# A planned transformer block on one core: where the empty steps go, who adds one tile of exponentials, and where a square root stands

## The chip, the cores and the metric

The kernel runs on one core of one Trainium2 chip. The time is device microseconds (us) from launch to end, as the median of three runs. Engines are called PE (TensorE), ACT (ScalarE), DVE (VectorE), POOL (GpSimd) and SP (SyncE, which here only issues DMAs).

## What is computed

x has 4 sequences of 2,048 tokens of 512 numbers, all fp32. With xn = layernorm(x), the output is x + attention(xn) + ffn(xn):

```
qkv  = xn @ qkv_w.T + qkv_b            # 16 heads of 32
attn = softmax(q @ k.T * 32**-0.5)     # over 2,048 keys
att  = (attn @ v) @ proj_w.T + proj_b
idx  = top2(xn[:, 0, :] @ Wr + br)     # two experts of eight per sequence
ffn  = mean over the two experts of gelu(xn @ W1[e] + b1[e]) @ W2[e] + b2[e]
out  = x + att + ffn
```

## The kernel before, in words

**Units and chunks.** Attention is cut into 64 *chunks*: a sequence b (4), a group g of four heads (4) and 512 queries qc (4). A chunk has 16 *units*, kt = 0 to 15, one for each 128 keys; there are 1,024 units, numbered U (chunk U // 16). For the four heads of a unit, PE brings minus the row maximum into PSUM (`shift`, L773), adds the scores (`score`, L781), and ACT takes the exponential into a tile `pT[U]` of 128x2048 (L918). The maxima come from a first pass 22 units ahead (`score_max`, L763, reduced by DVE, L925). At every even unit `weigh` (L793) multiplies the two units before by v, and DVE adds the result to `sacc` (L802).

**The sum over keys.** The softmax denominator needs the sum of the 16 tiles `pT` of a chunk. `add_weights` has POOL add them into `psums` (L816 for the first two, L820 for the next thirteen), and the sixteenth by a DMA that adds, issued from POOL (L818). In the next chunk, at kt 4 or 5 (`plan.keys_at`), `add_keys` sums `psums` over partitions with four matmuls by a tile of ones (L826); ACT copies the result into `sums`, DVE inverts it in four parts, POOL multiplies (`divide`, L887). The tiles `pT` have four buffers: the exponential of unit U+4 needs the buffer of unit U. In the last chunk most tiles are summed by PE (`add_last`), a few by POOL (L809, L811).

**The layers in between.** Each odd unit has room for one step of the other work ("item"), 32 matmuls as a rule, 16 for the first two steps of a layer: q/k projections ("qk"), v, expert layers ("w1", "w2"), output projection ("proj"). "qk" and "w1" use seven products of half blocks in place of eight. These need sums of blocks of tokens ("tx") and of weights ("ws"), which POOL makes, four for each of 14 places, at the last unit of a chunk and the first two of the next. A finished half of an expert's hidden layer gets its gelu on ACT in the unit after the next item but one (`curves`, L922), with a table load before it and one back to exp after it. Rows of the first sequence get a bias from POOL (L953); for the others POOL issues DMAs that add it (L699).

**The planner.** `Plan` fixes the "qk" and "v" items (for each chunk group at written-out slots), then fills the other odd units from two queues with earliest times. There are more slots than items: what is spare is dealt out to slots with kt 5 ("rests"), as empty slots ("gaps"), except where a gelu is due. If the slot at kt 5 is empty, the keys of the chunk before are summed there, else at kt 4. "stats", "normal" and "turn" (layernorm and transposition of the next sequence) and "root" (its square root: ACT with two table loads, DVE reciprocal, two POOL operations, L452 to L455) have fixed units too. Root stands at unit 129, 385 and 641 for sequences 1, 2 and 3.

**The order on an engine** is the order of issue in the loop over U: shift and scores, exponentials, gelu, maxima, inversion, `add_weights`, `weigh`, `add_last`, `add_keys`, extra steps, item, stores, loads. PSUM is a ring of eight banks for all of it. In the last chunk `add_last` for an even unit comes two units later, or three if that slot is empty:

```
            late = u + 3 < plan.units and u + 3 not in plan.items
            if u % 2 == 0 and u >= plan.units - NT and late == (u == U - 3):
                add_last(u)
```

Of the kernel before, what the change touches and what calls it, by code (L numbers as in the profile page):

```python
# [37 lines left out]
class Plan:  # L38
# [3 lines left out]

    def __init__(self, B, DC, NCH, NT, TPC):
        self.per_group = NCH * NT
        self.per_seq = DC * self.per_group
        self.units = B * self.per_seq
# [10 lines left out]
        for G in range(1, B * DC):  # L59
            b, g = divmod(G, DC)  # L60
            first = (G - 1) * self.per_group
            for n, products in enumerate(GAPS):
                at = (11, 12, 13, 14, 15, 16, 17, 19) if g else (5, 6, 7, 8, 9, 11, 12, 13)
                fixed[first + 2 * at[n] + 1] = ("qk", b, g, products)
            if g == 0:
                at = [n for n in range(14, 32) if n % 8 != 2]
# [10 lines left out]
        for b in range(1, B):  # L77
            q1 = (b - 1) * self.per_seq + self.per_group
            q2 = q1 + self.per_group
            for k in range(TOP_K):  # L80
                at = q1 + ((NT - 1, q2 - q1 + 5 * NT - 1) if b > 1 else (-1, NT - 1))[k]
                for n in range(4):
                    self.extra.setdefault(at + COMBINED[n], []).append(("ws", b, (k, n)))
                for i in STEPS:
                    self.first_load["wt", ("w1", b, k, i)] = at + STORED + 1
            for n in range(NT):
                self.extra.setdefault(q1 + 2 * (16 + n) + 1, []).append(("stats", b, n))
                c, i = divmod(n, TPC)
                at = q2 + 2 * (1 + 18 * (c // 2) + 5 * (c % 2) + i) + 1
                self.extra.setdefault(at, []).append(("normal", b, n))  # L90
                self.extra.setdefault(at + 2, []).append(("turn", b, n))
            self.extra.setdefault(q2 + 1, []).append(("root", b, 0))
            for p in range(NCH // 2):
                at = q2 + 2 * NT * (p + 1) - 1
                for n in range(4):
                    self.extra.setdefault(at + COMBINED[n], []).append(("tx", b, (p, n)))
                for i in STEPS:
                    self.first_load["xt", (b, p, i)] = at + STORED + 1
                for c in (2 * p, 2 * p + 1):
                    self.first_load["xq", (b, c)] = at + STORED + 1  # L100
# [35 lines left out]
        todo = len(fixed) + sum(len(p) for _, p in ffn + proj)  # L136
        spare = len(slots) - todo - 4
        free = [s for s in slots if s > 0 and s not in fixed]
        rests = [s for s in free if s % NT == 5]
        share = spare / len(rests)  # L140
        current, before, owed = [], None, 0
        for s in slots:
            if s in fixed:
                self.items[s] = [fixed.pop(s)]
                before = None
                continue
            curve = before is not None and (
                before[0] == "w1" and before[4][-1] in ((3, 0), (3, 1), (2, 1))
                or before[0] == "w2" and before[3] % 2 == 1 and before[5] == 0
            )  # L150
            before = None
            if s in rests:
                owed += share
                if owed > 0 and not curve:
                    owed -= 1
                    continue
            if not current:
                for queue in (proj, ffn):
                    if queue and queue[0][0] <= s:
                        current = queue.pop(0)[1]  # L160
                        break
            if current:
                before = current.pop(0)
                self.items[s] = [before]
        self.keys_at = {}
        for s in range(NT, self.units, NT):
            ends = s + NT == self.units
            self.keys_at[s // NT - 1] = 5 if s + 5 not in self.items and not ends else 4
        assert not fixed and not proj and not ffn and not current, (proj, ffn, current)

        rows_at = {}
# [27 lines left out]
        for u in range(2, self.units + 1, 2):  # L199
            kt, G = (u - 2) % NT, (u - 2) // self.per_group  # L200
# [45 lines left out]
def block_kernel(  # L246
# [17 lines left out]
    B, N, D = x.shape  # L264
    E = Wr.shape[1]
    DC = D // P
    NT = N // P
    NCH = N // CH
    TPC = CH // P
    SCALE = float(HD) ** -0.5  # L270
    PSUM = bass.MemoryType.PSUM
    plan = Plan(B, DC, NCH, NT, TPC)
# [11 lines left out]
    def bank(name):  # L284
        return ps.tile([P, CH], F32, tag="bank", name=name)

    def rows_of(j):
        return slice(j * HD, (j + 1) * HD)
# [454 lines left out]
    def place(u):  # L743
        rest, kt = divmod(u, NT)
        rest, qc = divmod(rest, NCH)
        return (*divmod(rest, DC), qc, kt)

    mx, negm, sacc, psums, sums, pT = {}, {}, {}, {}, {}, {}
# [55 lines left out]
    def add_weights(u):  # L804
        b, g, qc, kt = place(u)
        if u >= plan.units - NT:
            if kt == 3:
                psums[b, g, qc] = pair.tile([P, GH, CH], F32, tag="psum", name="psum_last")
                nc.gpsimd.tensor_tensor(psums[b, g, qc], pT[u - 1], pT[u], ALU.add)  # L809
            elif kt in (5, 7, 9):  # L810
                nc.gpsimd.tensor_tensor(psums[b, g, qc], psums[b, g, qc], pT[u], ALU.add)  # L811
        elif kt == 0:
            return
        elif kt == 1:
            psums[b, g, qc] = pair.tile([P, GH, CH], F32, tag="psum", name=f"psum_{b}_{g}_{qc}")
            nc.gpsimd.tensor_tensor(psums[b, g, qc], pT[u - 1], pT[u], ALU.add)  # L816
        elif kt == NT - 1:
            nc.gpsimd.dma_start(psums[b, g, qc], pT[u], accum_op=ALU.add)  # L818
        else:
            nc.gpsimd.tensor_tensor(psums[b, g, qc], psums[b, g, qc], pT[u], ALU.add)  # L820

    def add_keys(where, ps, weights, again):

        for n, t in enumerate(weights):
            for j in range(GH):
                nc.tensor.matmul(  # L826
                    ps[rows_of(j), :], ones, t[:, j, :],
                    start=(n == 0), stop=(n == len(weights) - 1),
                )
        if again:  # L830
            nc.vector.tensor_tensor(sums[where], ps, sums[where], ALU.add)
        else:
            last = where == place(plan.units - 1)[:3]
            sums[where] = pair.tile(
                [P, CH], F32, tag="vrow" if last else "sums", bufs=2 if last else 1,
                name="sums_%d_%d_%d" % where,
            )
            nc.scalar.activation(sums[where], ps, AF.Identity)  # L838

    def add_last(u):  # L840
        where, kt = place(u)[:3], place(u)[3]
        if kt == 2:
            return
        weights = [pT[u]] if kt in (4, 6, 8) else [pT[u], pT[u + 1]]
        if kt == 12:
            weights.append(psums[where])
        add_keys(where, bank(f"keys_{u}"), weights, kt > 0)
# [50 lines left out]
    for U in range(-LEAD, plan.units):  # L898
        second = U >= 0
        first_pass = U + LEAD if U + LEAD < plan.units else None  # L900
        chunk, kt = divmod(U, NT)
        b, g, qc, _ = place(U) if second else (0, 0, 0, 0)
# [16 lines left out]
        curve = curves.pop(U, None)  # L919
# [14 lines left out]
        before = place(U - NT)[:3] if U >= NT else None  # L934
# [8 lines left out]
        two = any(it[0] in ("qk", "w1") and len(it[-1]) == 2 for it in plan.items.get(U, []))  # L943
# [6 lines left out]
        if second:  # L950
            add_weights(U)
# [7 lines left out]
        for u in (U - 2, U - 3):  # L959
            late = u + 3 < plan.units and u + 3 not in plan.items  # L960
            if u % 2 == 0 and u >= plan.units - NT and late == (u == U - 3):
                add_last(u)
        if before is not None and kt == keys:
            add_keys(before, bank("keys_%d_%d_%d" % before), [psums[before]], False)
        for step, sb, n in plan.extra.get(U, []):
            if step == "stats":
                if n == 0:
# [9 lines left out]
            else:  # L977
                c, i = divmod(n, TPC)
# [2 lines left out]
                if i == TPC - 1:  # L981
                    later(U + 1, lambda sb=sb, c=c, xs=xs: nc.sync.dma_start(xn_dram[sb, c], xs))
        for item in plan.items.get(U, []):
            dense(item, U, curve is not None, invert if two else lambda: None)


        for do in waiting.pop(U, []):
# [30 lines left out]
    U = plan.units  # L1018
# [78 lines left out]
```

## Time and profile before

| what | value |
|---|---|
| median of 3 runs | 4973.19 us (4972.93 to 4974.06) |
| profiled execution | 4967.9 us, of it 4966.1 us span and 1.8 us around it |
| granted PE clock | 0.999 |
| PE busy | 4913.9 us (99%) |
| POOL busy | 4403.5 us (89%) |
| DVE busy | 3714.2 us (75%) |
| ACT busy | 2491.9 us (50%) |
| POOL adds of pT, L820 | 819, 4547 ns each |
| DMAs that add pT, L818 | 63, 1,024 KB each, 8.6 us median from issue to landing |

Busy time and a wait must be told apart here: PE is booked busy nearly always, since its matmuls are pipelined, so a short wait shows better in the distance between units than in a busy share. The first matmuls of L773 in each unit mark its start; all 4,096 of them are in the trace.

### The profile page before, as it was taken

The numbers are of one execution on the slowest core, as the hardware profiler recorded it, in microseconds if no ns is written. First come the engines' busy times: TensorE is split into PE (matmuls) and PEld (weight loads), VectorE is DVE, ScalarE is ACT, GpSimd is POOL, SyncE is SP. The second block draws the span as 40 slices with busy tenths as digits, with TensorE's granted clock in tenths as the row PEclk, the third lists the DMA queues.
The fourth block names the chain that finished last, engine by engine and source line by source line (L and its number), as shares of the span: only waits on it lengthen the run. The fifth ranks groups of instructions, "written<-read, shape, count | busy, mean of one in ns | idle before, by whom it ended". The sixth has DMA issues, their size and how long they took to land.

```text
span 4966.1 us, 108027 instructions
## 1 busy us (share of the span) xinstructions
PE 4913.9 (99%) x44740; PEld 1712.0 (34%) x44740; DVE 3714.2 (75%) x5899; ACT 2491.9 (50%) x4570; POOL 4403.5 (89%) x1469
## 2 busy tenths in 40 slices
PE   8999999999999999999999999999999999999999
PEld 2333333333333333333333333333333333333332
DVE  5777787777777787777777778877777777777772
ACT  1445456464444545454455445555544445555553
POOL 2799999999898998999988998999988988989983
PEclk9999999999999999999999999999999999999999
DMA  6334337433333434634234244564423343323323
GB/s 225 113 106 120 112 99 196 150 121 110 82 107 104 131 109 139 187 122 137 88 94 132 73 128 128 171 167 131 145 70 98 106 129 107 95 81 112 87 81 101
DMA packets 327772, 594.93 MB, mean 120 GB/s; under 512 B 42220, under 2 KB 162540, under 8 KB 310384
## 3 DMA queue, kind: packets, MB, share of 16 engines
q1 hardware_dynamic: 311872, 509.37, 31.7%
q0 software_dynamic: 15408, 78.65, 8.2%
q8 instruction: 352, 5.77, 0.5%
q14 instruction: 140, 1.15, 0.1%
HBM read 380.81 MB, written 153.62 MB: 108 GB/s over the span
## 4 chain that ended last, share of the span: by engine, by line
PE 83%; ACT 6%; POOL 5%; issue 3%; DMA 2%; DVE 1%; SPq 0%; POOLq 0%; ACTq 0%
PE acc L793 17%; PE s L781 15%; PE m L763 15%; PE qkps L503 6%; PE ops L503 6%; PE hps L503 6%; PE s L773 6%; PE vps L503 5%; POOL psum L820 4%; PE prps L503 4%; ACT p L918 3%; DMA psum<-p 2%; PE keys L826 1%; ACT L692 1%; ACT h L922 1%
## 5 line engine op out<-in xcount | busy, mean ns | idle before, releaser
L820 POOL TENSOR_TENSOR psum<-psum,p 128x2048 f32<-128x2048 f32 x819 | 3724.0, 4547 | 158.3 <-ACT p L918 117.4
L918 ACT ACTIVATE p<-s 128x512 f32<-128x512 f32 x4096 | 2116.9, 602 | 2225.3 <-PE m L763 2062.8
L925 DVE TENSOR_REDUCE mx<-m 128x1 f32<-128x512 f32 x4096 | 2543.1, 683 | 569.2 <-PE m L763 567.4
L781 PE MATMUL s<-qT,kT 32*128 32x512 f32 x8192 | 1919.0, 588 | 0.0
L763 PE MATMUL m<-kT,qT 32*128 32x512 f32 x8192 | 1911.3, 590 | 3.9 <-DVE row L657 2.5
L763 PEld LDWEIGHTS m<-kT,qT 32*128 32x128 f32 x8192 | 921.8, 184 | 330.2 <-issue 240.5
L793 PE MATMUL acc<-p,v 128*32 128x512 f32 x8192 | 985.8, 599 | 9.6 <-ACT p L918 5.5
L781 PEld LDWEIGHTS s<-qT,kT 32*128 32x128 f32 x8192 | 768.1, 185 | 30.8 <-issue 9.2
L503 PE MATMUL ops<-wb_w,h 128*32 128x512 f32 x4096 | 466.0, 595 | 0.2 <-ACT p L918 0.2
L816 POOL TENSOR_TENSOR psum<-p,p 128x2048 f32<-128x2048 f32 x63 | 288.1, 4573 | 194.0 <-ACT p L918 194.0
L793 PEld LDWEIGHTS acc<-p,v 128*32 128x32 f32 x8192 | 214.0, 109 | 709.7 <-ACT p L918 392.8
L802 DVE TENSOR_TENSOR sacc<-acc,sacc 128x512 f32<-128x512 f32 x448 | 309.9, 692 | 139.9 <-PE acc L793 139.9
L773 PE MATMUL s<-negms,ones_b 32*128 32x512 bf16 x4096 | 406.2, 385 | 7.5 <-ACT p L918 7.0
L503 PE MATMUL hps<-xt,wt_w 128*32 128x512 f32 x3584 | 411.0, 596 | 1.1 <-ACT p L918 1.0
L773 PEld LDWEIGHTS <-ones_b 32*128 32x128 bf16 x4096 | 103.4, 91 | 858.0 <-issue 850.4
L503 PE MATMUL qkps<-xt,wt_qk 128*32 128x512 f32 x3360 | 386.7, 597 | 11.4 <-ACT p L918 11.4
L940 DVE RECIPROCAL sums<-sums 128x128 f32<-128x128 f32 x252 | 235.9, 936 | 0.7 <-ACT sums L838 0.7
L503 PEld LDWEIGHTS ops<-wb_w,h 128*32 128x32 f32 x4096 | 120.0, 109 | 314.7 <-issue 229.8
L657 DVE SCALAR_TENSOR_TENSOR row<-ops,row 128x512 f32<-128x512 f32 x128 | 88.5, 691 | 163.9 <-PE ops L503 153.6
L503 PE MATMUL prps<-wb_proj,xl_at 128*32 128x512 f32 x1792 | 203.9, 595 | 0.0
L503 PEld LDWEIGHTS hps<-xt,wt_w 128*32 128x32 f32 x3584 | 103.3, 109 | 276.2 <-issue 185.4
L503 PEld LDWEIGHTS qkps<-xt,wt_qk 128*32 128x32 f32 x3360 | 97.1, 110 | 283.6 <-issue 180.6
(127 smaller groups left out, 1975.6 us busy)
## 6 DMA issues: line engine op xcount, KB each, us to landing
xt<-t_dram SPq DMA_DIRECT2D x181, 512.0 KB
xt<-xn_dram SPq DMA_DIRECT2D x133, 512.0 KB
psum<-p POOLq DMA_DIRECT2D x63, 1024.0 KB, 8.6
part_dram<-row SPq DMA_DIRECT2D x128, 256.0 KB
v_dram<-v SPq DMA_DIRECT2D x64, 256.0 KB
wt_w<-ws_dram SPq DMA_DIRECT2D x128, 128.0 KB
v<-v_dram SPq DMA_DIRECT2D x64, 256.0 KB
row<-part_dram SPq DMA_DIRECT2D x64, 256.0 KB
```

Of the source, the lines that this page charges most:

```text
L503: nc.tensor.matmul(pp[rows_of(j), :], lhsT[:, rows_of(j)], rhs, start=(first and n == 0), stop=(last and n == len(terms) - 1),)
L657: nc.vector.scalar_tensor_tensor(row, pp, 0.5, row, ALU.mult, ALU.add)
L763: nc.tensor.matmul(t, qT[b, g, qc][r, ts(i, P)], kT[b, g, kc][r, :], start=True, stop=True)
L773: nc.tensor.matmul(tiles[j], ones_b[r, :], negm[b, g, qc][r, :], start=True, stop=False)
L781: nc.tensor.matmul(tiles[j], kT[b, g, kt // TPC][r, ts(kt % TPC, P)], qT[b, g, qc][r, :], start=False, stop=True,)
L793: nc.tensor.matmul(acc[r, :], held["v", (b, g, kt // TPC)][:, (kt + n) % TPC, r], pT[u + n][:, j, :], start=(n == 0), stop=(n == 1),)
L802: nc.vector.tensor_tensor(t, acc, t, ALU.add)
L816: nc.gpsimd.tensor_tensor(psums[b, g, qc], pT[u - 1], pT[u], ALU.add)
L820: nc.gpsimd.tensor_tensor(psums[b, g, qc], psums[b, g, qc], pT[u], ALU.add)
L918: nc.scalar.activation(pT[U][:, j, :], tiles[j], AF.Exp, scale=SCALE)
L925: nc.vector.tensor_reduce(dst, t, AX.X, ALU.max, negate=True)
L940: nc.vector.reciprocal(sums[before][:, q], sums[before][:, q])
```

## The change

1. **Gaps.** A chunk in whose first units POOL sums blocks ("ws" or "tx" that begin at the last unit of the chunk before) gets no gap at kt 5. There are twelve such chunks; the same number of gaps is dealt to the rest.
2. **One tile of chunk 62.** For unit 1007, the sixteenth of the last chunk but one, `add_weights` does nothing (no adding DMA). PE sums that tile over partitions by ones at unit 1008, ACT copies it into `sums`; at kt 4 or 5 the rest of the chunk is summed as ever and DVE adds it to `sums`.
3. **Roots.** If the planner finds a root in a slot that it marks as a gelu's, it plans once more with that sequence's root, normals and turns two units later. In a unit with a root the first evacuation of a "w1" layer, a copy, goes to DVE in place of ACT.

Worked through with this kernel's sizes, the slots change so (gaps at kt 5 by chunk, and the empty slots of the last chunk by unit):

| | before | after |
|---|---|---|
| chunks with a gap | 0 1 4 5 7 9 11 13 15 16 18 20 22 24 26 28 30 33 34 35 37 39 42 43 45 47 48 50 52 54 57 58 60 62 | 0 1 6 7 8 9 13 14 16 17 19 20 23 24 30 31 32 33 35 38 39 41 43 47 48 50 51 53 54 56 57 60 61 62 |
| chunks that sum blocks | 4 5 10 12 21 26 28 29 37 42 44 45 | the same |
| empty in the last chunk | 1011, 1021, 1023 | 1011, 1013, 1023 |
| root of sequences 1, 2, 3 | 129, 385, 641 | 129, 387, 641 |
| gelu units near the second root | 385, 387 | 385, 387 |

Most items stay or move one slot earlier (2 units); a few change places with others.

```diff
@@ Plan.__init__
-    def __init__(self, B, DC, NCH, NT, TPC):
+    def __init__(self, B, DC, NCH, NT, TPC, late=()):
...
-                at = q2 + 2 * (1 + 18 * (c // 2) + 5 * (c % 2) + i) + 1
+                at = q2 + 2 * (1 + (b in late) + 18 * (c // 2) + 5 * (c % 2) + i) + 1
...
-            self.extra.setdefault(q2 + 1, []).append(("root", b, 0))
+            self.extra.setdefault(q2 + 1 + 2 * (b in late), []).append(("root", b, 0))
...
-        rests = [s for s in free if s % NT == 5]
+        summed = {
+            (s + 1) // NT for s, steps in self.extra.items() for e in steps
+            if e[0] in ("ws", "tx") and s % NT == NT - 1
+        }
+        rests = [s for s in free if s % NT == 5 and s // NT not in summed]
         share = spare / len(rests)
-        current, before, owed = [], None, 0
+        current, before, owed, curved = [], None, 0, set()
...
+            if curve:
+                curved.add(s)
...
+        again = {
+            b for s, steps in self.extra.items() for kind, b, _ in steps
+            if kind == "root" and s in curved
+        }
+        if again and not late:
+            self.__init__(B, DC, NCH, NT, TPC, tuple(again))
+            return
@@ add_weights
+        elif u == plan.units - NT - 1:
+            return
         elif kt == NT - 1:
             nc.gpsimd.dma_start(psums[b, g, qc], pT[u], accum_op=ALU.add)
@@ the loop over U
+        ends_soon = U >= plan.units - NT
+        if ends_soon and kt == 0:
+            add_keys(before, bank("keys_%d_%d_%d" % place(U)[:3]), [pT[U - 1]], False)
         if before is not None and kt == keys:
-            add_keys(before, bank("keys_%d_%d_%d" % before), [psums[before]], False)
+            add_keys(before, bank("keys_%d_%d_%d" % before), [psums[before]], ends_soon)
...
-            dense(item, U, curve is not None, invert if two else lambda: None)
+            rooted = any(e[0] == "root" for e in plan.extra.get(U, []))
+            dense(item, U, curve is not None or rooted, invert if two else lambda: None)
```

## The prediction

> **What bounds the kernel now.** I read the page first (busy shares, chain), then ACT's waits, then the timeline around the longest of them, and last the distances between the first L773 matmuls of neighbouring units, all 1,024 of them.
>
> ```profile
> span 4966.1 us, 108027 instructions
> PE 4913.9 (99%) x44740; PEld 1712.0 (34%) x44740; DVE 3714.2 (75%) x5899; ACT 2491.9 (50%) x4570; POOL 4403.5 (89%) x1469
> ...
> L820 POOL TENSOR_TENSOR psum<-psum,p 128x2048 f32<-128x2048 f32 x819 | 3724.0, 4547 | 158.3 <-ACT p L918 117.4
> ...
> psum<-p POOLq DMA_DIRECT2D x63, 1024.0 KB, 8.6
> ```
>
> PE is the bound. The change removes no PE work, so it can only remove waits of PE. How much waiting is there? From the unit distances: an even unit takes 3.90 us when nothing disturbs it (478 of them), an odd one with a full item 5.61, with a half item (16 matmuls) or a gap 1.72 or 3.57 less, keys add 0.86. Against those numbers units 0 to 1022 lose some 80 us in all, of it 0.43 at each of the 33 gaps with keys at kt 5 (0.14 in the gap, 0.29 after it). The losses of half a us and more are few, and of three kinds.
>
> *Kind 1, the adding DMA.* The exponential at kt 3 needs the buffer of kt 15 of the chunk before, which the DMA reads:
>
> ```profile
> ACT p L918 <- DMA psum<-p: 33.9, 8, 8.4
> ```
>
> ACT's timeline at the last chunk, and then POOL's, show the worst case:
>
> ```profile
> 4870.41 2.06 ACT L918 ACTIVATE p<-s 128x512 f32<-128x512 f32 x4 [2.69 <-PE s L781]
> 4880.86 2.07 ACT L918 ACTIVATE p<-s 128x512 f32<-128x512 f32 x4 [8.39 <-DMA psum<-p]
> ```
>
> ```profile
> 4863.81 4.57 POOL L820 TENSOR_TENSOR psum<-psum,p 128x2048 f32<-128x2048 f32 x1
> 4868.67 0.87 POOL L818 DMA_DIRECT2D psum<-p  x1 [0.30 <-POOL psum L820]
> ```
>
> POOL issues the DMA 8.76 us after the exponential of unit 1007 ended (its *lag*), the chain of waits gives the DMA 12.09 us, and unit 1012 takes 12.20 us where 3.90 is its due: 8.30 lost. For the other chunks I set lag plus landing time beside the loss: 17.0 (chunk 60) loses nothing, 17.7 (37) 0.61, 17.9 (44) 0.78, 18.3 (57) 1.41, 18.8 (5) 1.70, 23.0 (28) 7.43. So **17.0 us is the allowance**; past it PE loses about the excess, a little more if it is large. Losses of this kind: 5: 1.70, 7: 3.70 (1.51 of it at unit 128, where POOL itself is late), 9: 1.11, 22: 1.17, 28: 7.43, 37: 0.61, 42: 0.81, 44: 0.78, 57: 1.41; sum 18.7, and 8.30 at the end.
>
> *Kind 2, root with gelu*, ACT at unit 385:
>
> ```profile
> 1951.28 1.28 ACT L922 ACT_TABLE_LOAD   x1
> 1952.58 1.06 ACT L922 ACTIVATE h<-h 128x1024 f32<-128x1024 f32 x1
> 1953.65 1.28 ACT L692 ACT_TABLE_LOAD   x1
> 1954.95 0.20 ACT L692 ACTIVATE unused<-ones 128x1 f32<-128x1 f32 x1
> 1955.17 1.28 ACT L452 ACT_TABLE_LOAD   x1
> 1956.46 0.31 ACT L452 ACTIVATE sd<-mv,eps 128x16 f32<-128x16 f32 x1
> 1956.79 1.28 ACT L692 ACT_TABLE_LOAD   x1
> 1958.08 0.20 ACT L692 ACTIVATE unused<-ones 128x1 f32<-128x1 f32 x1
> ```
>
> Seven us between two exponentials; unit 386 loses 3.31. Unit 388, after a gelu with a normal, loses 0.81.
>
> *Kind 3, DVE or ACT crowded*: units 102 (0.78), 106, 378 and 618 (1.25 each) after "w1" or "qk" steps with three DVE evacuations beside statistics or an inversion; 380, 620, 142, 434, 654 (0.77 to 0.87) around gelus.
>
> **The change, part by part.**
>
> *Chunk 62 by PE.* Taken away: DMA and POOL's issue. At unit 1008 four matmuls come (eight records): 0.86 us by the L826 rows of the same size. They wait for nothing new: `weigh` ahead of them in unit 1008 already reads tile 1007. The ACT copy (0.60 to 0.63 us, L838) queues ahead of exponential 1009, where ACT idles 0.97; if that cover were gone it would cost its length. The DVE add takes 0.69 (L831) in place of the copy at kt 4, ahead of the inversion at kt 5, with DVE mostly idle there. POOL's last add ends at 4868.37, so keys at kt 4 (4875) find it done. The wait of 8.30 goes; next late is exponential 1010's buffer, free 2.0 us before its need. So −8.30 + 0.86 = −7.4.
>
> *The gap at 1013 in place of 1021.* At 1021 two postponed tiles of `add_last` (1.72 us of PE) fill the gap; at 1013 the postponed call is the one for kt 2, which does nothing. PE then has only 1.19 us in that unit, while ACT needs 2.06 for each exponential: `weigh` at 1014 waits for exponential 1013. ACT starts 1.34 after a unit's start, so 1012 runs 1.34 to 3.41 and 1013 to 7.30; PE gets there at 3.90 + 1.19 + 1.19 = 6.27: 1.0 to 1.15 lost (between 0 if banks let PE run differently, and 2.1, one whole exponential). I take +1.1. **Tail: −6.3.**
>
> *Gaps moved.* A gap shortens a chunk by 3.57 − 0.43 = 3.1 us net (0.4 is spent again on the gap itself) and adds about that to POOL's lag if POOL is busy throughout. What the gaps themselves cost, and the total of gaps, is as before. By chunk, lag from a running sum (old lag + POOL's work − PE's time), landing as measured before in that chunk:
> - 28 (four half items, token blocks): before 2.1 + 77.6 − 66.9 = 12.8; after, 3.3 longer without its gap, 9.5; landing 10.2: excess 6.0 → 2.7; loss 7.4 → 3.4.
> - 5: no gap in 4 and 5, lag 10.7 → about 5: 1.70 → 0. 37: 9.0 → 6: 0.61 → 0. 42: 0.81 → 0.
> - 22 loses its gap without summing blocks: landing was 12.0, lag 4.3 → 2.5: 1.17 → 0.
> - 7: row biases on POOL, one or two 1.3 us adds fewer, as they move to 6; chunk 1.7 shorter by a half item. Lag 9.9 → 8.2 to 9: 3.7 → 0.7.
> - 9 keeps its gap, but 8 gets one: lag 7.5 → 8.5: 1.1 → 2.1.
> - 41 gets a gap and has the bias DMAs as 9 has: before 5.0 + 77.3 − 76.4 = 5.9; after 3.2 (chunk 40 has 1.8 more PE work) + 77.3 − 72.8 = 7.7; landing 10.6: 0 → 1.2. Bounds: 0, and 3.1 (its whole lost length).
> - 38 gets a gap, landing there was 13.2: 0 → 0.9. 44 and 57 stay: 0.8 and 1.4.
> New sum 10.5 against 18.7: **−8.2**. Landing times are the weak point: they ran from 6.9 to 13.2 us and depend on loads that move. Bounds −12 and −2.
>
> *Roots.* The plan moves root 2 from 385 to 387, but the gelu's second half stands at 387 in both plans: root again follows a gelu, the same 6.9 us, and the loss of 3.31 moves to unit 388. Gained is only that the normal leaves that unit: −0.8. [...] The row shows the load alone; gelu starts 0.02 us after it. [...] With root really apart it would be −3.3 by the row. The copy on DVE at 129 and 641 (about 0.7 us by L657, in place of 0.6 on ACT behind root's 3.1 us) lies under a half item of 1.86 us: 0, bounds ±0.7.
>
> *Items one slot earlier.* Units 102, 106 and 620 lose their crowding (−2.5); similar steps land beside inversions or gelus in chunks 5, 29 and 37 and at 431; nearest rows 0.26 to 0.87 each: +2.3. Six more xt or wt loads of the plan's 869 are on SP; xt loads issued two units before use occur in both plans (six before, two after), and no unit of before waits on one; two wt loads become that short: 0, bounds 0 and +3. **Together with roots −1.0**, bounds −4 and +4.
>
> **Sum.** −6.3 − 8.2 − 1.0 = −15.5. The profiled execution, 4967.9 (span 4966.1 + 1.8), would take 4952.4. The median runs 5.3 above the profiled one, so I predict 4957.7, rounded to **4958**.
>
> **The rivals.** About 0.2% (10 us) is what this kernel's measurement can tell from no change: faster means below 4963.2, slower above 4983.1.
> - A, as summed, 4953 to 4963: 0.52.
> - B, only the tail pays; new landings and crowding take back what the gaps give: 4973.2 − 6.3 = 4967: 0.18. For it: landing varies by 6 us from chunk to chunk. Against: the 28, 5 and 37 sums are large.
> - C, more: landings are shorter once POOL is on time, and crowding leaves without coming back: −6.3 − 12 − 4 gives 4951: 0.15.
> - D, the tail does not do what it says: the wait at 1012 is taken over by another buffer or bank. Then −8.2 − 1.0 + 2.0 gives 4966: 0.08. Against: the next buffer is free 2 us early.
> - E, slower: POOL's lag carries from gap to gap. After, 16 gap chunks directly follow another gap chunk, before 7 (1 and 62 aside). If POOL no longer caught up at each chunk's head, each could lose 1.6: 16 × 1.6 = 26, giving 4984. It decides once lag at a chunk's end exceeds some 9 us, for then POOL's idle time before the add at kt 1 (3 to 9 us now) is gone. Against: 34, 35 and 48 follow a gap chunk and lag 4.4, just like 18 and 30. 0.07.
>
> So faster 0.67, same 0.26, slower 0.07. Range 4950 to 4967: A, most of C, and B and D to their middle.
>
> **What would show it.** Unit 1012 at 3.9 us, no ACT wait of 8 us on psum<-p, 62 such DMAs; unit 1014 about 1 us long over its due. Unit 467 loses 2.7 to 4, 99 and 371 nothing, 675 about 1. Unit 388 loses 3.3: if it doesn't, my reading of the roots is wrong. I am wrong if L918's waits on psum<-p stay above 25 us in all, or if new units with 2 us and more appear in chunks 6 to 9, 31 to 33 or 38 to 41.

## The result, and the profile after

The changed kernel takes 4964.54 us (median of 16 runs, 4959.88 to 4967.52) against 4973.48 us before (16 runs, 4970.38 to 4978.18): ratio 0.998, interval 0.9974 to 0.9987. That is 8.9 us or 0.18% less, inside the range of the prediction and somewhat over half of the forecast 15.5. It is above the 4963.2 below which the prediction would have called the kernel faster: the case "same", to which it gave 0.26. The profiled execution took 4965.18 us, 4963.4 of it span.

First the page of the changed kernel. Its lines have moved: L933 is the exponential, L835 POOL's add, L833 the adding DMA, L806 `weigh`, L516 the items, L465 to L468 root, L937 the gelu.

```profile
span 4963.4 us, 108069 instructions
PE 4916.5 (99%) x44748; PEld 1713.5 (35%) x44748; DVE 3717.3 (75%) x5904; ACT 2489.0 (50%) x4566; POOL 4402.9 (89%) x1468
...
L835 POOL TENSOR_TENSOR psum<-psum,p 128x2048 f32<-128x2048 f32 x819 | 3724.4, 4547 | 155.7 <-ACT p L933 114.7
...
psum<-p POOLq DMA_DIRECT2D x62, 1024.0 KB, 8.5
```

One DMA and one POOL issue fewer, eight matmul records more, and otherwise the same shares: a page cannot tell such kernels apart. ACT's waits and its timeline at the tail can:

```profile
ACT p L933 <- DMA psum<-p: 20.4, 6, 5.9
```

```profile
4875.91 2.07 ACT L933 ACTIVATE p<-s 128x512 f32<-128x512 f32 x4 [2.69 <-PE s L794]
4878.94 2.06 ACT L933 ACTIVATE p<-s 128x512 f32<-128x512 f32 x4 [0.97 <-PE s L794]
```

These are the exponentials of units 1010 and 1011, whose starts stood 10.45 us apart before and stand 3.03 apart now. The stretch from unit 1008 to the end (the tail) went from 104.87 to 97.51 us. But the waits on the DMA fell by 13.5 us in all, more than the tail gave, and the longest left is 5.9. It is new, at unit 131, in the head of chunk 8; the prediction had named a new loss of 2 us or more in chunks 6 to 9 as a sign that it is wrong. The changed kernel's timeline there, POOL's issue, then ACT, then PE:

```profile
751.80 0.86 POOL L833 DMA_DIRECT2D psum<-p  x1 [0.30 <-POOL psum L835]
...
761.89 2.07 ACT L933 ACTIVATE p<-s 128x512 f32<-128x512 f32 x4 [5.92 <-DMA psum<-p]
762.54 5.34 PE L516 MATMUL hps<-xt,wt_w 128*32 128x512 f32 x32 [4.01 <-ACT p L933]
```

PE waits 4.0 us, and then its 32 matmuls take 5.34 in place of 3.64. The losses of units against their due, found as in the prediction, in two profiles of each kernel (the second ones come with the experiments):

| units | before | before, again | after | after, again |
|---|---|---|---|---|
| 88 and 600 | 0 | 0 | 3.75 | 3.75 |
| 99 | 1.70 | 1.85 | 0 | 0 |
| 102, 106, 620 | 2.80 | 2.81 | 1.13 | 1.12 |
| 128, 130, 131 | 3.78 | 3.88 | 6.92 | 8.01 |
| 371 | 1.17 | 1.20 | 1.65 | 1.34 |
| 386, 388 | 4.12 | 4.12 | 5.00 | 5.11 |
| 399, 400 | 1.10 | 1.56 | 2.71 | 2.79 |
| 467 | 7.43 | 8.93 | 4.26 | 1.00 |
| 642, 643 | 0.07 | 0.07 | 1.21 | 2.72 |
| all of units 1 to 1007 | 71.2 | 73.0 | 75.2 | 73.6 |
| unit 1008 to the end | 104.87 | 105.71 | 97.51 | 97.51 |

So in the profiles the tail gave what the change gave, and over the first 1,008 units gains and losses cancel.

### The profile page after: what moved, and what is told of

Same layout as the page of the kernel before. It is cut to its first block, busy times and chain, and to the rows that moved or that the text cites. A ratio compares the mean times of both kernels' runs of the same rounds, so it can differ in the third digit from the quotient of the medians.

```text
span 4963.4 us, 108069 instructions
## 1 busy us (share of the span) xinstructions
PE 4916.5 (99%) x44748; PEld 1713.5 (35%) x44748; DVE 3717.3 (75%) x5904; ACT 2489.0 (50%) x4566; POOL 4402.9 (89%) x1468
## 4 chain that ended last, share of the span: by engine, by line
PE 86%; ACT 6%; POOL 3%; DMA 2%; issue 1%; DVE 1%; SPq 0%; POOLq 0%; ACTq 0%
PE acc L806 18%; PE s L794 16%; PE m L776 15%; PE qkps L516 7%; PE hps L516 7%; PE ops L516 6%; PE s L786 6%; PE vps L516 5%; PE prps L516 4%; POOL psum L835 3%; ACT p L933 3%; PE keys L841 1%; DMA psum<-p 1%; ACT L705 1%; ACT h L937 1%
## 5 line engine op out<-in xcount | busy, mean ns | idle before, releaser
L835 POOL TENSOR_TENSOR psum<-psum,p 128x2048 f32<-128x2048 f32 x819 | 3724.4, 4547 | 155.7 <-ACT p L933 114.7
L933 ACT ACTIVATE p<-s 128x512 f32<-128x512 f32 x4096 | 2116.6, 602 | 2227.7 <-PE m L776 2076.3
L806 PE MATMUL acc<-p,v 128*32 128x512 f32 x8192 | 986.7, 599 | 11.2 <-ACT p L933 7.3
L516 PE MATMUL ops<-wb_w,h 128*32 128x512 f32 x4096 | 466.0, 595 | 0.5 <-ACT p L933 0.5
L806 PEld LDWEIGHTS acc<-p,v 128*32 128x32 f32 x8192 | 214.2, 109 | 710.8 <-ACT p L933 395.6
L516 PE MATMUL hps<-xt,wt_w 128*32 128x512 f32 x3584 | 412.7, 598 | 5.7 <-ACT p L933 5.7
L516 PE MATMUL qkps<-xt,wt_qk 128*32 128x512 f32 x3360 | 387.0, 598 | 5.2 <-ACT p L933 2.7
L516 PEld LDWEIGHTS ops<-wb_w,h 128*32 128x32 f32 x4096 | 120.0, 109 | 315.0 <-issue 229.9
L516 PE MATMUL prps<-wb_proj,xl_at 128*32 128x512 f32 x1792 | 203.9, 595 | 0.2 <-ACT p L933 0.2
L516 PEld LDWEIGHTS hps<-xt,wt_w 128*32 128x32 f32 x3584 | 103.7, 110 | 282.9 <-issue 186.5
L516 PEld LDWEIGHTS qkps<-xt,wt_qk 128*32 128x32 f32 x3360 | 97.5, 110 | 276.4 <-issue 180.3
```

Source lines behind the costliest of these rows:

```text
L516: nc.tensor.matmul(pp[rows_of(j), :], lhsT[:, rows_of(j)], rhs, start=(first and n == 0), stop=(last and n == len(terms) - 1),)
L806: nc.tensor.matmul(acc[r, :], held["v", (b, g, kt // TPC)][:, (kt + n) % TPC, r], pT[u + n][:, j, :], start=(n == 0), stop=(n == 1),)
L933: nc.scalar.activation(pT[U][:, j, :], tiles[j], AF.Exp, scale=SCALE)
```

## The experiments

Times are medians; ratios are to the kernel before on the same chip, with their interval. Some kernels share the same runs of before. Times of versions that did not run together compare less well.

**One part at a time.** `tail_only`: the kernel before, with PE summing the tile of unit 1007.

```diff
+        elif u == plan.units - NT - 1:
+            return
...
+        if ends_soon and kt == 0:
+            add_keys(before, bank(...), [pT[U - 1]], False)
```

> Only the second part of the change, on the kernel before: PE adds the last tile of the last chunk but one, the planner as before (the gap of the last chunk stays at unit 1021). Theory (nearly all of the change's 8.9 us comes from here, since in the two profiles the stretch from unit 1008 on is 104.9 us before and 97.5 after): 7 to 7.5 us under before, about 4966, unit 1012 at 3.9 us. Rival (the moved gaps give the 8 us of the prediction, and the tail pays little in an average run, its DMA being late only in the one profile shown): 2 us or less under before, about 4972.

Measured: 4964.92 against 4972.73, ratio 0.9984 (0.9977 to 0.9991), 7.8 us less. Unit 1012 is at its due, the tail 97.43 us. The theory holds. The gap of the last chunk stays at 1021 here, so what this answers to in the prediction is the −7.4 of the keys.

`gaps_only`: the kernel before, with the planner's new rule for gaps.

```diff
-        rests = [s for s in free if s % NT == 5]
+        rests = [s for s in free if s % NT == 5 and s // NT not in summed]
```

> Only the first part, on the kernel before: no gap in chunks that sum blocks. Tail and roots as before. Theory (what the gaps free at units 99, 467 and 611 is taken back by a larger loss at the head of chunk 8 and by new crowding at units 88 and 600): 0 to 3 us under before, about 4972. Rival (the gaps give what the prediction said): 8 us under before, about 4965. The gap that moves from unit 1021 to 1013 changes the tail by up to 1 us either way in both.

Measured: 4972.76, ratio 0.9999 (0.9990 to 1.0007). The gaps alone gain nothing (this version also moves the items and the gap to 1013). Unit 99 loses nothing, as forecast, and 467 loses 5.34 us where 2.7 to 4 was forecast; but 130 and 131 lose 5.94, 88 and 600 1.9 each, and 642 and 643 3.90, where root now shares a unit with a layer's first step.

`roots_only`: the kernel before, with the third part (later root, DVE copy).

```diff
-                at = q2 + 2 * (1 + 18 * (c // 2) + 5 * (c % 2) + i) + 1
+                at = q2 + 2 * (1 + (b in late) + 18 * (c // 2) + 5 * (c % 2) + i) + 1
-            self.extra.setdefault(q2 + 1, []).append(("root", b, 0))
+            self.extra.setdefault(q2 + 1 + 2 * (b in late), []).append(("root", b, 0))
...
-            dense(item, U, curve is not None, ...)
+            dense(item, U, curve is not None or rooted, ...)
```

> Only the third part, on the kernel before: the planner moves the second root two units on, and in a unit with a root the first evacuation of a layer goes to DVE. Theory (root lands on the gelu's second half; unit 388 loses 4.8 where 386 and 388 lost 3.3 and 0.8; the DVE copy at unit 129 costs or saves about 1): 0 to 2 us over before, about 4974.5. Rival (the third part is what took back the gaps' gain): 5 us over before or more, about 4979.

Measured: 4975.17, ratio 1.0003 (0.9995 to 1.0012): no difference that can be told. Unit 388 loses 4.90 in place of 386's 3.31 and its own 0.81: root has only changed the gelu that it collides with. 399 and 400 lose 2.8, as in the changed kernel, where `gaps_only` loses 0.6: this loss comes with the third part.

**Where root stands.** `root_apart`: the changed kernel, root, normals and turns of sequence 2 two units later still.

```diff
-                at = q2 + 2 * (1 + (b in late) + 18 * (c // 2) + 5 * (c % 2) + i) + 1
+                at = q2 + 2 * (1 + 2 * (b in late) + 18 * (c // 2) + 5 * (c % 2) + i) + 1
-            self.extra.setdefault(q2 + 1 + 2 * (b in late), []).append(("root", b, 0))
+            self.extra.setdefault(q2 + 1 + 4 * (b in late), []).append(("root", b, 0))
```

> The changed kernel with one difference: the second root, its normals and turns come four units later than before and not two, so that root stands at unit 389, where no gelu is. Theory (the loss of 4.8 us at unit 388 is root queued behind a gelu on ACT): 4 to 5 us under the changed kernel's 4964.5, about 4960, and units 386 to 390 within 0.5 us of their due. Rival (ACT is crowded there by the normals and turns, root or no root): within 1 us of the changed kernel, with the loss at 390 or later.

Measured: 4961.43, ratio 0.9975 (0.9965 to 0.9986), 11.3 us under before where the changed kernel was 8.9 under. The intervals of the two overlap. The theory was half right: 388 is at its due, but unit 390 loses 4.00. ACT's timeline shows why, between the exponentials of units 389 and 390:

```profile
1974.35 2.06 ACT L933 ACTIVATE p<-s 128x512 f32<-128x512 f32 x4 [1.73 <-PE m L776]
1976.28 0.63 ACT L853 ACTIVATE sums<-keys 128x512 f32<-128x512 f32 x1
1976.92 1.28 ACT L465 ACT_TABLE_LOAD   x1
...
1979.95 2.04 ACT L933 ACTIVATE p<-s 128x512 f32<-128x512 f32 x4
```

Unit 389 is a gap with key sums, 3.04 us of PE; 0.63 of copy and 3.0 of root after an exponential have no cover there. In the profile this version also gains 2.7 us at 399 and 400 (there PE waits in the changed kernel 1.70 us for the load of `negms`, the row maxima; why the load is late there and not here isn't shown) and loses 2.1 more at 371 and 1.3 at 675. So the profile shows no gain to speak of, and the 2 us by which the time is lower stay open.

`root_at_item`: root at 391, under a full item. With root so late the last block of tokens of sequence 2 is stored when POOL has begun to form block sums in it, so what the later layers read of it is changed; the instructions are the same.

```diff
+                at = q2 + 2 * (1 + 3 * (b in late) + 18 * (c // 2) + 5 * (c % 2) + i) + 1
+            self.extra.setdefault(q2 + 1 + 6 * (b in late), []).append(("root", b, 0))
```

> The changed kernel, but the second root with its normals and turns six units later than before and not two: at unit 391, an odd unit with a full item, no gelu, no key sums. Theory (a root takes 3.1 us of ACT between two exponentials, which a unit of 5.6 us covers and the empty unit 389 of 3.0 us did not): units 386 to 392 within 0.5 us of their due, 4 to 5 us under the changed kernel by that, about 4960, and 1 to 2 us under the version with root at 389. Rival (some such loss follows root wherever it stands): a loss of 3 us or more at 392, time as with root at 389.

Measured: 4964.94, ratio 0.9984 (0.9975 to 0.9992). Units 386 to 398 are within 0.25 us of their due, so a full item does cover root, as the theory said. The time did not fall, for unit 404 loses 7.68. The same loss in the `joined` version below, from ACT's timeline:

```profile
2038.40 0.81 ACT L473 ACTIVATE xl_normal<-xl_normal,nb,sd 128x512 f32<-128x512 f32 x1 [4.72 <-DMA xl_normal<-in_x_dram]
2039.12 0.58 ACT L556 ACTIVATE h<-hps 128x512 f32<-128x512 f32 x1
2039.60 2.05 ACT L934 ACTIVATE p<-s 128x512 f32<-128x512 f32 x4
```

A normal waits 4.7 us on ACT for its rows of x, loaded into the only buffer just as POOL issues the four bias DMAs of 1,024 KB, and the exponential stands behind it. That the bias DMAs are what delays the load is an inference from their nearness in time.

`copy_on_act`: the changed kernel without the DVE copy at roots.

```diff
-            dense(item, U, curve is not None or rooted, ...)
+            dense(item, U, curve is not None, ...)
```

> The changed kernel, but in a unit with a root the first evacuation of a layer stays on ACT. Theory (at unit 641 the copy queues behind root on ACT and PE waits for its bank: unit 642 loses 3.1 us as with the gaps alone, against 1.1; at 130 and 131 about 5.9 against 6.9): 0 to 2 us over the changed kernel, about 4965.5. Rival, as in the prediction (the copy lies under its half item): no difference, unit 642 at 1.1 us or less in both.

Measured: 4962.87, ratio 0.9980 (0.9973 to 0.9987), the same as the changed kernel within the scatter. In the profile unit 642 loses 2.19 in place of 1.14, and 130 and 131 together 5.84 in place of 6.92: the copy on DVE saves about one us at one root and costs one at the other (four profiles with these gaps and the copy lose 6.8 to 8.0 at 130 and 131, the two without it 5.8 and 5.9). Neither theory's 0 to 2 us can be told from none in the time.

**The adding DMA.** `two_more`: the changed kernel, PE summing the sixteenth tile of chunks 7 and 28 as well.

```diff
+BY_PE = (7, 28, 62)
...
-        elif u == plan.units - NT - 1:
+        elif kt == NT - 1 and u // NT in BY_PE:
             return
...
-        ends_soon = U >= plan.units - NT
+        ends_soon = chunk - 1 in BY_PE
```

> The changed kernel, and the sixteenth tile of chunks 7 and 28 too is summed by PE in the unit after (as the change does for chunk 62), 0.86 us of PE each. Theory (units 131 and 467 wait for the adding DMA, 5.8 and 4.3 us in the changed kernel's profile, half-speed PE after the wait included): both waits go, 10.0 - 1.7 = 8.3 us under the changed kernel's 4964.5, about 4956, and no half-speed stretch near 131 and 467. Rival (POOL itself or the normals of sequence 1 hold PE there): 131 stays over 3 us late, and the time within 4 us of the changed kernel.

Measured: 4961.41, ratio 0.9980 (0.9971 to 0.9989). In the profile both waits are gone (131 and 467 at 0) and the losses of units 1 to 1007 fall from 75.2 to 68.3; PE pays 1.7. The times show 3 us less at most, which the intervals don't settle. Part of the difference is that 467 lost only 0.9 to 1.0 in three later profiles of kernels with the same gaps, not 4.3. There the theory had the wrong cause: most of the 4.3 was a late load of `xt` (below), and only 0.7 the adding DMA.

`joined`: root at 391 (with the same changed block of tokens), and tiles 7, 22, 28 and 62 on PE.

```diff
-BY_PE = (7, 28, 62)
+BY_PE = (7, 22, 28, 62)
```

> The changed kernel with root at unit 391 and PE summing the sixteenth tile of chunks 7, 22, 28 and 62. Theory: 8.3 us for chunks 7 and 28, 0.8 or more for chunk 22 (unit 371 lost 1.0 to 3.8 in the profiles so far, less 0.86), 4 to 5 for root: 13 to 15 us under the changed kernel, about 4950.5, and below every version so far. Rival (losses move on to the next tight chunk): no more than 8 us under the changed kernel.

Measured: 4956.77, ratio 0.9971 (0.9964 to 0.9978), 7.8 under the changed kernel by the medians. Of its 22 executions one took 4989 us and one 10652, for reasons that no trace shows. In the profile 131, 371 and 388 are at their due, and unit 404's 7.3 us is about what is missing from the theory's 13 to 15.

`joined_fixed`: the normals re-placed so that the load of x has time, and chunk 57 on PE too.

```diff
+                at = q2 + 2 * (1 + (b in late) * (3, 4, 1, 1)[c] + 18 * (c // 2) + 5 * (c % 2) + i) + 1
...
-BY_PE = (7, 22, 28, 62)
+BY_PE = (7, 22, 28, 57, 62)
```

> As the joined version (root at unit 391), but the normals and turns of sequence 2 so placed that its second block of tokens comes eight units later than in the kernel before, the first six, the last two as in the changed kernel; and PE sums the sixteenth tile of chunk 57 too (7, 22, 28, 57, 62). Theory (unit 404 of the joined version lost 7.3 us since a normal waited on ACT for its load of x, queued behind the bias DMAs; two more units give the load its time; chunk 57's wait of 1.4 to 2.2 us goes for 0.86): unit 404 and 406 within 1 us of their due, about 4948.5. Rival (the load is late for another reason, or the loss moves to the turns and block sums of that sequence at units 411 to 417): a loss of 4 us or more between 404 and 420, about 4956.

Measured: 4947.51 us (4945.85 to 4950.31), ratio 0.995 (0.9937 to 0.9964): 24 us under before, the fastest version, with the last block of tokens stored in time again. Its page begins:

```profile
span 4944.1 us, 108130 instructions
PE 4911.0 (99%) x44780; PEld 1712.9 (35%) x44780; DVE 3720.0 (75%) x5908; ACT 2488.6 (50%) x4566; POOL 4398.3 (89%) x1464
```

PE runs 32 records more than in the changed kernel and is booked 5.5 us less. Matmuls at half the clock are booked longer (5.34 for 3.64 us above): the record of the granted clock has three half-speed stretches of 3.41 us in the changed kernel (units 131, 388 and 467) and here none but the one at the very end (mean granted clock 0.999 there, 1.000 here), some 5 us of busy time by that record. Units 131, 371, 388, 404, 467 and 931 all lose 0.2 us or less; units 1 to 1007 lose 54.8 us in all.

**A wider rule for gaps.** `gaps_plus`: the changed kernel, and no gap where POOL adds row biases or issues bias DMAs.

```diff
-        rests = [s for s in free if s % NT == 5 and s // NT not in summed]
+        rests = [s for s in free if s % NT == 5 and s // NT not in summed | {7, 9, 25, 41}]
```

> The changed kernel, with no gap either in the chunks where POOL adds row biases or issues the bias DMAs (7, 9, 25, 41); by the new plan root stands at unit 387 with a full item and no gelu. Theory (131 lost 5.8 us since chunk 7 had both a gap and POOL's row biases; root alone costs nothing under a full item): 131 under 1.5 us, 388 under 0.5, about 8 us under the changed kernel, 4956.5. Rival (a new plan moves the losses to other chunks): within 3 us of the changed kernel, with new losses of 3 us or more elsewhere.

Measured: 4964.42, ratio 0.9986 (0.9979 to 0.9993). Both theories are half right: 131 loses 1.59 (1.14 more at 130) and 388 nothing, as the first said; but unit 403 loses 4.63, 691 3.59, 51 1.35, all new, and the time is that of the changed kernel. Moving gaps moves losses.

**The same kernels again.** `after_again` and `before_again`, unchanged.

> The changed kernel once more. Theory (what differs from run to run is how long the adding DMAs take to land[...]): the losses at fixed units 88, 378, 600, 618, 642, 1014 repeat within 0.1 us, those at 131, 371, 467, 931 differ by up to 3 us; the median within 2 us of 4964.5. Rival (the scatter is spread over all units): losses at 88, 600 and 642 differ by over 0.5 us as well.

Measured: 4964.80. 88, 378, 600, 618 and 642 repeat within 0.01 us; 467 lost 1.00 against 4.26, 131 6.87 against 5.78, 643 1.58 against 0.07. The theory holds, though 643 was not on its list. As to its 3.4 us: the wait of PE at 404 in `joined` was 3.45 and slow matmuls followed it, but at 467 they followed one of 2.49 in the first profile.

> The kernel before once more. Theory (its profile shown was a lucky one, 5.6 us under the median of its 16 runs): the losses before unit 1008 come to 74 to 79 us in place of 71.2, the difference at 130, 386 and 467, where a wait in some runs halves PE's clock; the tail from unit 1008 on is 104.9 us again. Rival: 71 us again, the unprofiled runs being longer for a reason that the profile does not show.

Measured: 4972.39, ratio 1.0001; losses before unit 1008 73.0, between the two expectations, with only 467 clearly longer (8.93). The tail was 105.7. That the first profile of before was a lucky one explains 1.8 of its 5.6 us there and 0.8 in the tail; the rest stays open, and this second profile, too, is that of the fastest of its ten runs.

## Why the prediction came out so

That the number lay in the range is in part luck: the tail paid a little more than forecast, and what the gaps and the moved items were to give over the rest mostly did not come; the range was wide enough for that case. In us, by the means of the two profiles of each kernel:

| term | predicted | measured |
|---|---|---|
| tail | −6.3 | −7.8 |
| gaps: waits at the heads of chunks, 467 whole | −8.2 | −3.6 |
| items one slot earlier | −0.2 | +3.2 |
| roots: units 386, 388, 399 and 400 | −0.8 | +2.3 |
| sum | −15.5 | −5.9 |

The medians differ by 8.9, 3 us more than these profiles; that stays open.

**The tail: right, a little small.** With the gap left at 1021, `tail_only`, the keys' −7.4 measured −7.8. The keys of tile 1007 cost their 0.86 and no wait took the place of the old one. The term that was off is the empty unit 1013: 1.1 predicted, 0.31 lost at 1014. `weigh` multiplies tile 1012 first, four matmuls of 0.86 us in all, and only the second half needs tile 1013; I had let all of it wait.

**The gaps: the step "new sum 10.5 against 18.7: −8.2" failed.** Chunk 5 (−1.7 predicted, −1.8 measured) was right. The term that broke it is chunk 7: 0.7 predicted, 6.9 and 8.0 measured. Lag and landing were near what I took (8.7 and 10.0 us), so it was the allowance. It is the PE time from the exponential of kt 15 to that of kt 3, and I took 17.0 us for every chunk. A half item at kt 15 or kt 1 shortens it by 1.7. After the change half items stand at both (127 and 129): 13.6, and the excess is 18.7 − 13.6 = 5.1, not 1.7; half-speed matmuls behind the wait, 1.7 us, make 6.8 of it. The same sum explains chunk 22, where I expected nothing and got 1.3 to 1.7 (half items at 367 and 369: 2.5 + 12.7 − 13.6 = 1.6). My own row for it before already spoke against the 17.0: 4.3 + 12.0 = 16.3 lost 1.17, for the half item at 369 stood there too, which allows only 15.3. The half items were in the plan that I had before me. `two_more` and `joined_fixed` confirm the cause: with these tiles on PE the waits are gone.

The 3.7 that I booked as chunk 7's loss before was misread as well. The sum gives 9.9 + 9.0 − 15.3 = 3.6 there, but no exponential waited for that DMA: PE had lost 1.51 us at unit 128 and 2.19 at unit 130 to other waits, and the DMA, issued as below, landed 9.0 us later, 0.1 before the exponential of 131. From the timelines of POOL and ACT before:

```profile
750.18 0.86 POOL L818 DMA_DIRECT2D psum<-p  x1 [0.30 <-POOL psum L820]
759.24 2.07 ACT L918 ACTIVATE p<-s 128x512 f32<-128x512 f32 x4 [2.41 <-PE m L763]
```

So two delays lay one over the other. In the changed kernel 128 loses nothing and 130 1.14, and the second showed.

Chunk 28 came out near its number by luck. The DMA landed in 8.6 us, not 10.2, so its excess was 0.7, not 2.7; but a load that I had put at nothing was late in the same unit (below), and 467 lost 4.26 in one profile and 1.00 in the other where I had said 3.4.

**The clock behind a wait was missing.** I wrote "a little more if it is large". Two kernels with the same plan there, before and `tail_only`, show what it is. Both wait for root in unit 386; the windows are each one's wait and the 3.6 us behind it (columns: window, busy time of PE, PEld, DVE, ACT, POOL, granted clock, DMA share, GB/s). Before:

```profile
1951.50:1958.70 7.20, 5.12 (x40) 1.48 (x32) 2.11 (x5) 7.10 (x10) 4.87 (x3) 1.00 0.93 280
1958.70:1962.30 3.60, 3.56 (x37) 1.35 (x36) 2.24 (x5) 1.87 (x5) 1.99 (x1) 1.00 0.33 97
```

With the tail alone changed:

```profile
1955.00:1962.20 7.20, 5.08 (x44) 1.50 (x39) 2.15 (x5) 7.10 (x10) 4.61 (x3) 1.00 0.95 288
1962.20:1965.80 3.60, 3.60 (x20) 0.79 (x20) 1.26 (x3) 1.28 (x3) 2.24 (x1) 0.53 0.31 81
```

PE waited 2.08 us on DVE in both, and `weigh` after it, from the two PE timelines:

```profile
1958.82 1.93 PE L793 MATMUL acc<-p,v 128*32 128x512 f32 x16
```

```profile
1962.07 3.40 PE L793 MATMUL acc<-p,v 128*32 128x512 f32 x16
```

The second ran at half the clock, for 3.41 us by the record of the granted clock, and lost 4.78 us where the first lost 3.31. The wait was of the same length in both, so its length alone does not tell which of the two comes; what does was not shown. Slow matmuls stand behind other waits too: in the changed kernel at 131 (4.01 us of wait, then a granted clock of 0.50 over 3.4 us) and at 388 (2.07 us, then 0.50 over 3.41 us; 4.83 lost, not my 3.3), in `joined` at 404 (3.45 us, then 3.64 us of `weigh` in place of 1.92) and in `root_apart` at 390 (2.13 us, then 3.50 of `weigh`). A long wait of PE thus cost its length and, where the clock fell, about 1.5 us more (at 386 4.78 against 3.31; at 131 the 1.70 of the 32 matmuls).

**Roots: right that the collision stays**, wrong by 1.7 on its price (−0.8 predicted, +0.9 in the profiles), by that clock. And 399 and 400, after the later normals, lose 1.4 more, which I had put at nothing. The copy at roots was costed at nothing; it moves one us from 642 to 130 and 131.

**Items one slot earlier: the other step that failed, −0.2 against +3.2.** The relief came (102, 106 and 620: −1.7). In its place units 88 and 600 lose 1.87 each: a gelu in a unit with a half item leaves ACT 3.90 us for an exponential and 3.8 us of gelu. I had taken 0.3 to 0.9 from units with full items. 642, where the root of sequence 3 now shares its unit with a layer's first step, loses 1.1. And what I took from "no unit of before waits on one", of loads issued two units before use, failed at 467, from the PE timeline of the changed kernel:

```profile
2352.70 5.34 PE L516 MATMUL qkps<-xt,wt_qk 128*32 128x512 f32 x32 [2.49 <-DMA xt<-t_dram]
```

That load was issued at 465 for 467; PE waits for it again in the second profile, 0.93 us. The matmuls of 5.34 us ran at half the clock (granted clock 0.50 over 3.41 us of them; 3.64 in the second profile).

Of the rivals B, only the tail pays, says what came: 4967 against 4964.5. D has the nearer number, 4966, but its cause is not in the trace: 1012 is at its due and nothing took over its wait. E did not come: chunks 31 to 33 each follow a gap chunk with lags of 4.4, 4.2 and 7.9, about 33's 7.8 before.

## What to carry to other kernels

When a buffer is handed round through a slow helper, compare its delay with the busy engine's own time between release and reuse, chunk by chunk: filler that is half as long there shortens that time (1.7 us here) as surely as a gap does (3.6). A delay that costs nothing may only be hidden behind another one. A planner that moves empty slots away from one conflict must cost what they meet in the new place, and half-length items count as half a gap. Where a few places lose more than the work costs on the busy engine, move the work there: 0.86 us of PE removed waits of up to 8 us with no change of plan.

## What the runs showed of the hardware

- A wait of PE of 2.08 us at one and the same place of the program (unit 386) was followed by a granted clock of 1.00 over 3.6 us in the profile of before and of 0.53 in that of `tail_only`; what decides was not shown. The half-speed stretches of the changed kernel at 131, 388 and 467 were 3.41 us long, the one of before at 1012 was 6.83, and that of `tail_only` cost 1.47 us of work (`weigh` 3.40 in place of 1.93).
- The same 1,024 KB adding DMA from SBUF to SBUF landed in 6.9 to 13.2 us within one execution. One chunk had nearly the same time in two runs of one kernel (chunk 28's: 10.2 twice before, 8.6 twice after; in `gaps_only` 11.0), so it goes with the plan; which of the traffic beside it sets it was not tried.
